# Attention of a graph layer by pairs of graphs: four-row-tile scores, and DRAM transposes whose read is issued apart from the write

## Chip, cores and metric

One core of a Trainium2 chip runs the whole program. The metric is the device time of one execution in microseconds, as the median of the runs. All data is float32. A float32 matmul of the program stands as two MATMUL and two LDWEIGHTS instructions in the trace, so counts in the profile are twice those of the code.

## The reference

There are 128 graphs of 128 nodes with 256 features, and an adjacency matrix of 0 and 1 for each. Two layers follow each other. Layer 0 is a graph attention network and a feed-forward block; layer 1 is a relational attention with 8 heads of 32 and four relations, and another feed-forward block:

```python
h = _gat(_gat(x, adj, W1, a1), adj, W2, a2)        # layer 0, softmax over masked scores
h = _layernorm(x + h); x = _layernorm(h + relu(h @ w_ff1 + b_ff1) @ w_ff2 + b_ff2)
...
q, k = heads(src @ Wq + bq), heads(src @ Wk + bk)  # layer 1
attn = softmax(q @ k^T / sqrt(dh))                 # 8 heads, 128 x 128 per graph and head
for r in range(4):
    v_r = heads(src @ Wv[r] + bv[r])
    out = out + (attn * (adj_matrix == r)) @ v_r
x = _ln(src + out @ Wo + bo)
x = _ln(x + gelu(x @ W1 + b1) @ W2 + b2)
```

With adjacencies of 0 and 1 alone the relations 2 and 3 select nothing, and the kernel takes its BINARY branch: one mask and two value tensors per graph. A GENERAL branch for other adjacencies is in the program and does not run here.

## The kernel before

**Tiling.** The 128 graphs are 32 groups of `G` = 4. A group goes through five stages, each a Python generator: `load`, `gat` (two graph attentions), `ff0`, `att` (the attention of layer 1) and `ff1`. The token tile `y` has 128 nodes on the partitions and 4 x 256 features.

**Order of the work.** `layers` keeps a heap of due times. Group g starts a stage at 100·g plus the `begin` of the stage, in units of its own; each `yield TIMES[...]` says after how many units the stage goes on. The emission order that comes out of the heap is pinned for TensorE (from unit 280 on) and for SyncE (from 0 on), which issues every DMA. TensorE and SyncE therefore work through a list in a fixed order, each at the speed that its waits allow; a unit is no time on the chip. The order on VectorE, ScalarE and GpSimd is left to the compiler's scheduler. In the steady state five groups are in flight, each in another stage.

**Transposes by DRAM.** Away from the first and last groups, a transpose of a 128 x 1024 tile is a 32 x 32 block transpose on VectorE (L288), four DMAs of 128 KB that write the blocks to a DRAM tile `zd` (L291), and one DMA of 512 KB that reads it back in the new order (L293). `transposed` issues all five in a row on SyncE; the read waits there until the writes have landed. `features` makes the transposed features `hT` of a group this way for `ff0`, `att` and `ff1`, and `turned` does it for the attention weights `e` of a graph. `gat_weighting` sends one row of sums through DRAM in the same manner (L405, L407).

**Attention.** `qT` and the keys come from `hT` by L468 and L474. The keys are written twice by ScalarE into the constant tiles `kbd` (L476), each time with the rows of every other head multiplied by zero, so that one 64-row tile of TensorE serves two heads: the scores of a graph are 4 matmuls of 64 rows x 256 columns (L490), two row tiles at a time, into two PSUM banks. `weights(b)` then takes maxima (VectorE, L496), 8 exponentials with sums (ScalarE, L500), reciprocals (L501) and the product on GpSimd (L502). `by_relation` masks the transposed weights (L515), `values` makes the value tensors (L531, L532), `weighted` sums over 32-column tiles, four at a time (L544), and L577/L578 apply `Wo` and add to `y`. The graphs of a group are staggered: `weights(b + 2)` stands right behind `weighted(b)`.

**The second half of a feed-forward block** is L378, in three blocks of TensorE work, the last of which closes `y`; `normalised` (L256 to L265) follows, and then the next stage's `features`. PSUM has 7 banks under the name `mm` and one under `av`.

## Time and profile before

| what | value |
|---|---|
| median of 3 runs (range) | 2890.71 us (2889.82 to 2892.4) |
| the profiled execution | 2891.83 us; its span 2890.0 us |
| TensorE matmul / weight load busy | 2787.7 us (96%) / 2166.1 us (75%) |
| VectorE / ScalarE / GpSimd busy | 1504.7 / 1724.3 / 1597.4 us (52 / 60 / 55%) |
| DMA queue, share of 16 engines | 49.1% |
| L490, scores: union of matmuls | 147.7 us, x1024 |
| L544, weighted sums: union of matmuls | 107.3 and 104.6 us, x2048 each |

Busy time is a union over the span; a matmul's end is modelled, so that the start of one block and the start of the next say more than the durations. "PE" is TensorE's matmul, "PEld" its weight load, "SPq" SyncE's issuing of DMAs. In a timeline view the columns are start and duration in us, engine, line, operation, output and inputs, shape and count, and in brackets the idle time before it with what ended it.

### The profile page before, as it was taken

How to read it: one execution, taken by the hardware profiler on the slowest of the kernel's cores; microseconds unless marked ns; L12 is line 12 of the kernel's file. 1: busy time of each engine (PE TensorE's matmuls, PEld its weight loads, DVE VectorE, ACT ScalarE, POOL GpSimd, SP SyncE). 2: the span in 40 equal slices, each digit the busy share in tenths (PEclk: the TensorE clock that was granted, in tenths of full speed). 3: DMA queues.
4: the chain of work that ended last, by engine and by line, in shares of the span. 5: the costliest groups of instructions: out<-in, count | busy, mean ns of one | idle time of the engine just before them, and what ended most of it. 6: DMA issues, size and time to landing. Idle time of an engine off the chain costs nothing.

```text
span 2890.0 us, 45554 instructions
## 1 busy us (share of the span) xinstructions
PE 2787.7 (96%) x15554; PEld 2166.1 (75%) x15554; DVE 1504.7 (52%) x3072; ACT 1724.3 (60%) x5191; POOL 1597.4 (55%) x1866
## 2 busy tenths in 40 slices
PE   4996999999999999999999999999999999999988
PEld 3764777777877777777777787777778777777756
DVE  5444545545545555554554555555565545555442
ACT  3445566566666666666656666666666675666543
POOL 1434556556655556665655665565566565556553
PEclk7998999999999999999999999999999999999999
DMA  7145454555554556555445545454654544564310
GB/s 275 45 104 121 104 118 106 110 132 127 119 114 107 113 117 139 114 119 118 106 108 131 129 113 125 104 111 117 137 128 107 123 106 111 122 135 106 77 37 15
DMA packets 1156945, 328.69 MB, mean 114 GB/s; under 512 B 903008, under 2 KB 1126752, under 8 KB 1156064
## 3 DMA queue, kind: packets, MB, share of 16 engines
q1 hardware_dynamic: 1156704, 325.68, 49.1%
q8 instruction: 126, 2.06, 0.3%
q14 instruction: 115, 0.94, 0.1%
HBM read 195.97 MB, written 129.62 MB: 113 GB/s over the span
## 4 chain that ended last, share of the span: by engine, by line
PE 71%; DMA 7%; DVE 6%; POOL 5%; ACT 4%; issue 2%; SPq 2%; DVEq 0%; POOLq 0%; ACTq 0%
PE mm L378 25%; PE mm L333 19%; PE mm L531 5%; PE mm L474 4%; PE mm L468 4%; PE mm L490 4%; PE av L544 3%; PE mm L435 3%; PE mm L577 3%; POOL tok L271 2%; DMA zd<-e 2%; SPq L291 2%; DMA eT<-zd 2%; PE mm L454 1%; DMA zd<-T 1%
## 5 line engine op out<-in xcount | busy, mean ns | idle before, releaser
L271 POOL TENSOR_TENSOR tok<-tok,ln_rows 128x512 f32<-128x512 f32 (+1 forms) x596 | 669.5, 1133 | 34.4 <-PE mm L282 11.1
L500 ACT ACTIVATE e<-mm,nm 128x128 f32<-128x128 f32 x1024 | 362.1, 397 | 239.2 <-DVE nm L496 229.6
L378 PE MATMUL mm<-w,fT 128*128 128x256 f32 x2048 | 460.6, 381 | 0.0
L378 PE MATMUL mm<-wf,fT 128*128 128x256 f32 x2048 | 456.6, 381 | 1.5 <-ACT fT L354 1.5
L378 PEld LDWEIGHTS mm<-w,fT 128*128 128x128 f32 x2048 | 386.6, 190 | 74.2 <-issue 24.2
L502 POOL TENSOR_TENSOR e<-e,s 128x512 f32<-128x512 f32 x256 | 269.4, 1053 | 300.5 <-DVE s L501 299.8
L378 PEld LDWEIGHTS mm<-wf,fT 128*128 128x128 f32 x2048 | 386.5, 190 | 64.3 <-issue 9.2
L515 DVE TENSOR_TENSOR m<-eT,am 128x1024 f32<-128x1024 f32 x128 | 186.2, 1454 | 385.2 <-DMA eT<-zd 374.8
L496 DVE TENSOR_REDUCE nm<-mm 128x4 f32<-128x512 f32 x256 | 162.9, 676 | 254.6 <-PE mm L490 254.6
L265 ACT ACTIVATE tok<-tok,nmr,rstd 128x256 f32<-128x256 f32 x480 | 249.9, 603 | 20.1 <-POOL nmr L263 20.0
L531 PE MATMUL mm<-wv,T 128*128 128x512 f32 x512 | 249.3, 610 | 0.0
L352 POOL TENSOR_TENSOR fT<-fT 128x512 f32<-128x512 f32 x128 | 163.3, 1277 | 153.8 <-ACT fT L351 153.8
L500 ACT ACTIVATION_READ_ACCUMULATOR e<-mm,nm 128x1 f32 x1024 | 242.9, 237 | 0.0
L354 ACT ACTIVATE fT<-fT,col 128x512 f32<-128x512 f32 x256 | 170.4, 715 | 118.8 <-DVE fT L348 117.1
L309 POOL TENSOR_TENSOR t<-T 128x256 f32<-128x256 f32 x64 | 47.6, 744 | 321.3 <-DMA T<-zd 321.0
L333 PE MATMUL mm<-T,w 128*128 128x256 f32 x768 | 202.3, 386 | 4.0 <-DMA T<-zd 2.9
L424 POOL TENSOR_TENSOR e<-e,s 128x512 f32<-128x512 f32 (+1 forms) x68 | 68.1, 1002 | 244.4 <-DVE s L423 230.6
L333 PE MATMUL mm<-T,wf 128*128 128x256 f32 x768 | 193.1, 381 | 0.0
L256 DVE BATCH_NORM_STATS2 st<-tok 128x6 f32<-128x256 f32 x480 | 176.7, 409 | 2.4
L333 PEld LDWEIGHTS mm<-T,w 128*128 128x128 f32 x768 | 144.4, 192 | 30.6 <-issue 6.5
L422 ACT ACTIVATE e<-e,nm 128x128 f32<-128x128 f32 x256 | 101.6, 430 | 105.2 <-DVE nm L419 98.8
L333 PEld LDWEIGHTS mm<-T,wf 128*128 128x128 f32 x768 | 146.1, 191 | 21.7 <-issue 0.8
(144 smaller groups left out, 5147.1 us busy)
## 6 DMA issues: line engine op xcount, KB each, us to landing
zd<-e SPq DMA_DIRECT2D x496, 128.0 KB, 4.6
eT<-zd SPq DMA_DIRECT2D x124, 512.0 KB, 4.4
zd<-T SPq DMA_DIRECT2D x364, 128.0 KB, 3.5
T<-zd SPq DMA_DIRECT2D x91, 512.0 KB, 4.2
xt<-in_xT_dram SPq DMA_DIRECT2D x32, 512.0 KB, 5.0
e<-zsd SPq DMA_DIRECT2D x60, 256.0 KB, 3.3
tok<-in_x_dram SPq DMA_DIRECT2D x30, 512.0 KB
out_dram<-tok SPq DMA_DIRECT2D x29, 512.0 KB, 5.4
```

Source lines behind the costliest of these rows:

```text
L256: nc.vector.bn_stats(st, y[:, b])
L265: nc.scalar.activation(y[:, b], y[:, b], AF.Identity, bias=nmr[:, b:b + 1], scale=rstd[:, b:b + 1])
L271: engine.tensor_tensor(y[:, b:b + n], y[:, b:b + n], v[:, None, :].to_broadcast([P, n, D]), op)
L333: nc.tensor.matmul(p[:, i], win[k][:, ts(f0 + i, P)], hs[k], start=first and i == 0, stop=True, skip_group_check=True)
L352: nc.gpsimd.tensor_add(hi[:, :, 1], hi[:, :, 1], hi[:, :, 0])
L354: nc.scalar.activation(lo[:, i], lo[:, i], func, bias=bin_[:, f0 + i:f0 + i + 1])
L378: nc.tensor.matmul(ys[b // 2][:, b % 2], fT[f][:, ts(b, N)], wout[:, f], start=b % 2 == 0 and n == 0, stop=n == FC - 1, skip_group_check=True)
L496: nc.vector.tensor_reduce(nm, p, AX.X, OP.max, negate=True)
L500: nc.scalar.activation(eh[:, q], p[:, q], AF.Exp, bias=nm[:, q:q + 1], accum_out=s[:, q:q + 1])
L502: nc.gpsimd.tensor_mul(eh, eh, per_row(s, N))
L515: nc.vector.tensor_tensor(m, eT, at[:, b][:, None, :].to_broadcast([P, H, N]), OP.mult)
L531: nc.tensor.matmul(p, hT[:, b, f], wv[:, f, r:r + 2], start=f == 0, stop=f == DC - 1)
```

## The change

1. Attention works on pairs of graphs (`together` = 2): `weights`, `turned`, `weighted` and the `Wo` product take two graphs at a time. A group has two steps in place of four, and the second pair's scores stand right behind the first pair's weighted sums.
2. The keys are written once, to a tile `kT`; `kbd`, `own` and `bk_own` go. The scores are 8 matmuls per graph of 32 rows x 128 columns, one per head, in four row tiles with a PSUM bank each; a pair uses four banks of `mm`.
3. `transposed` is split into `put` (block transpose and writes) and `get` (the read). The read is issued 7 units after the writes; a pair's second read 3 units after its first. In `gat_weighting` the read comes 5 units after the write.
4. Due times change: 48 units from a pair's scores to its weighted sums, `gat` and `load` begin 10 units earlier, row and attention of the graph attention network have 13 and 22 units, and the leads of `ff0`, `att` and `ff1` are cut by the 7 units that `put` takes. `m` has two buffers.

```diff
-    "ff first half": 10, "ff half": 5, "row": 16, "gat": 19, "wh": 5.5,
-    "gat copy": 2, "qk": 4.5, "scores": 5.5, "turn0": 10, "turn1": 5,
-    "v0": 5.5, "av": 9, "v": 4, "wo": 4, "turn": 3, "mask": 3,
-    "lead ff0": 26, "lead att": 32, "lead ff1": 32, "affine": 7,
+    "ff first half": 10, "ff half": 5, "row": 13, "gat": 22, "wh": 5.5,
+    "gat copy": 2, "qk": 7, "scores": 18, "mask": 7, "av": 13, "wo": 8, "turned": 10,
+    "put": 7, "next put": 3, "row put": 5,
+    "lead ff0": 19, "lead att": 25, "lead ff1": 25, "affine": 7,
...
-    period=100, bufs=dict(T=5, tok=5, m=1, mm=7, v=2),
-    begin=dict(load=-87, gat=-51, ff0=48, att=132, ff1=300),
+    period=100, bufs=dict(T=5, tok=5, m=2, mm=7, v=2),
+    begin=dict(load=-97, gat=-61, ff0=48, att=132, ff1=300),
...
-        nc.sync.dma_start(t, s.rearrange("k p i t -> p k (i t)"))
+        return s
+
+    def get(t, s):
+        if s is not None:
+            nc.sync.dma_start(t, s.rearrange("k p i t -> p k (i t)"))
...
-        transposed(y.rearrange("p b (c f) -> p (b c) f", f=P), blocks, direct, blocks)
+        s = put(y.rearrange("p b (c f) -> p (b c) f", f=P), blocks, direct, blocks)
+        yield TIMES["put"]
+        get(blocks, s)
...
-            for q in range(2):
-                nc.scalar.activation(c.kbd[i][:, :, q], p, AF.Identity, scale=c.own[:, q:q + 1],
-                                     bias=c.bk_own[q][:, i:i + 1])
+            nc.scalar.activation(kT[:, i], p, AF.Identity, bias=c.col["bk"][:, i:i + 1])
...
+            scores = [ps.tile([P, n, DC, N], F32, name="mm") for _ in range(HC)]
+            for j, b in enumerate(bs):
+                for i in range(DC):
+                    for q in range(HC):
+                        rows = ts(q, DH)
+                        nc.tensor.matmul(scores[q][:, j, i], qT[rows, i, ts(b, N)], kT[rows, i, ts(b, N)],
+                                         start=True, stop=True, tile_position=(q * DH, 0))
...
+        es = weights(range(STEP))
         yield TIMES["scores"]
+        eT = yield from turned(es)
+        for b in range(0, G, STEP):
+            bs = range(b, b + STEP)
+            vs = [values(k) for k in bs]
+            affine(y, "02", b, STEP)
+            yield TIMES["mask"]
+            parts = [(by_relation(k, e, range(R)), v) for k, e, v in zip(bs, eT, vs)]
             yield TIMES["av"]
+            oT = weighted(parts)
+            if b + STEP < G:
+                es = weights(range(b + STEP, b + 2 * STEP))
             yield TIMES["wo"]
+            p = ps.tile([P, STEP, D], F32, name="mm")
+            for j in range(STEP):
+                for i in range(DC):
+                    nc.tensor.matmul(p[:, j], oT[:, j, i], c.wo[:, i], start=i == 0, stop=i == DC - 1)
+            nc.vector.tensor_add(y[:, b:b + STEP], y[:, b:b + STEP], p)
+            if b + STEP < G:
+                yield TIMES["turned"]
+                eT = yield from turned(es)
```

## The prediction

> **What bounds the kernel now.** I read the page's busy times first, then the waits of TensorE, the windows of a period's length, and the timelines of the engines in one period.
>
> ```profile
> PE 2787.7 (96%) x15554; PEld 2166.1 (75%) x15554; DVE 1504.7 (52%) x3072; ACT 1724.3 (60%) x5191; POOL 1597.4 (55%) x1866
> ...
> PE mm L443 <- POOL e L424: 16.2, 4, 8.9
> PE av L544 <- DMA eT<-zd: 14.6, 2, 12.0
> ...
> 170.00:255.00 85.00, 64.16 (x404) 42.46 (x404) 37.57 (x72) 37.06 (x137) 19.80 (x25) 0.90 0.50 110
> ...
> 340.00:425.00 85.00, 85.00 (x482) 66.42 (x481) 44.27 (x93) 53.60 (x162) 50.02 (x58) 1.00 0.52 116
> ...
> 2805.00:2890.00 85.00, 66.51 (x338) 54.03 (x336) 22.12 (x49) 32.24 (x67) 33.38 (x42) 0.90 0.09 25
> ```
>
> TensorE is busy all the time and waits for others in a handful of places. From 340 to about 2690 us a window of 85 us holds 85.00 us of matmuls at a granted clock of 1.00; only the filling (20.8 us idle between 170 and 255) and the end have holes. No other engine passes 54 of 85 us. So in the middle the order list of TensorE sets the time, and what shortens it shortens the kernel, until a wait appears.
>
> ```profile
> 1403.62 7.07 PE L378 MATMUL mm<-w,fT 128*128 128x256 f32 x32
> 1410.62 1.14 PE L490 MATMUL mm<-kbd,T 64*128 64x256 f32 x8
> 1411.68 0.43 PE L544 MATMUL av<-eT,v 128*32 128x128 f32 x8
> 1411.92 0.40 PE L544 MATMUL av<-m,v 128*32 128x128 f32 x8
> 1412.14 0.40 PE L544 MATMUL av<-eT,v 128*32 128x128 f32 x8
> 1412.36 0.40 PE L544 MATMUL av<-m,v 128*32 128x128 f32 x8
> 1412.69 1.14 PE L490 MATMUL mm<-kbd,T 64*128 64x256 f32 x8
> 1413.76 3.72 PE L378 MATMUL mm<-w,fT 128*128 128x256 f32 x16
> ```
>
> Starts are read here, not durations. A full-array instruction of 256 columns takes 7.00/32 = 0.218 us (1403.62 to 1410.62). A graph's scores take 1.06 us (1410.62 to 1411.68; 1412.69 to 1413.76) for 8 instructions that run two abreast, so 4 rounds of 0.218 and 0.19 of filling and emptying. A graph's weighted sums take 1.01 us (1411.68 to 1412.69) for 32 instructions, four abreast: 0.22 us per 8, so 0.109 per round of four, and 0.14 besides.
>
> **One period, added up.** A group has 240 instructions of L333 and L378 (52.0 us), 6.9 for L468 and L474, 6.9 for L531, 3.5 for L577, 7.0 for the graph attention, 4.2 of scores and 4.0 of weighted sums: 84.5. The block of the same kind starts again 85.05 us later (1403.62 and 1488.67), so about 0.6 us goes to the four places per period where the full array gives way to smaller tiles and comes back, 0.15 each.
>
> **The edits on TensorE.** *Scores.* A pair has 32 instructions of 32 rows and 128 columns in four row tiles, 8 rounds. Four column tiles do a round in 0.109 us (L544), and the full array holds that pace with 128 columns of weights per instruction too:
>
> ```profile
> 124.72 0.94 PE mm L282 x8
> ```
>
> So a pair costs 8 x 0.109 + 0.19 = 1.06 us where two graphs cost 2.12: 2.1 us less per group. No row shows four row tiles. Its bounds are rounds of four at 0.109 (1.06 per pair) and one instruction after another (32 x 0.109 + 0.19 = 3.7 per pair, 3.1 us more per group); I take the first, since L490 does run its two row tiles abreast, weight loads too. A rule speaks against taking all of it: the Trainium skill, "TensorE: Matmul & The Clock Gate", section "Measured speedup vs the span model", gives four row tiles 3.07 times the speed of one instead of 4. By that, as an estimate, a pair would take 1.33 us and 0.5 us less would be saved per group; the sum goes by the rows above.
>
> *Weighted sums.* A pair is one block of 16 rounds: 16 x 0.109 + 0.14 = 1.88 instead of 2.02, 0.28 us per group. *Changes of tile size.* By the due times the second pair's sums (unit 67) stand right before the next group's first scores (71), and the first pair's sums right before the second pair's scores (19): two departures from the full array, not four, 0.3 us. Together 2.7 us: a period of 85.05 - 2.7 = 82.35.
>
> **Edits off TensorE.** The keys' copies fall from four per group to two (L476: 92.6 us busy in all, so 46 less on ScalarE); maxima and exponentials stay in number, reciprocals halve, GpSimd's product is one of twice the size. None of it is on the path while ScalarE has 31 us free per period. What it does is make bursts: 16 exponentials for a pair.
>
> ```profile
> 1412.51 0.37 ACT L500 ACTIVATE e<-mm,nm 128x128 f32<-128x128 f32 x1 [5.94 <-DVE nm L496]
> ...
> 1412.87 0.36 ACT L500 ACTIVATE e<-mm,nm 128x128 f32<-128x128 f32 x1
> ```
>
> One follows another by about 0.35 us, the first 1.9 us after the scores start. So a pair's four banks are held for 1.9 + 16 x 0.35 = 7.5 us. TensorE's list behind the first scores is half of the last feed-forward part (3.5), L577 (1.7), the first visit of the next one (1.7), the other half (3.5): the visit that needs the fifth and sixth bank comes 11.4 us after them. 3.9 us of cover; I charge nothing. If it fails (the graph attention's exponentials, 1.5 us, can come ahead, and more), each us over is paid once per period, 28 us in all. The rule that row tiling raises the pressure on PSUM (the Trainium skill, "TensorEngine Tiling (Array Packing)", "Gotcha 1: PSUM Pressure") speaks for such a wait; no row of this trace shows one, and by the rule alone no sum can be made.
>
> From a pair's scores to its sums TensorE has 37 to 41 us of other work. The chain needs 1.9 + 5.6 of exponentials, 2.1 (L502 twice), 1.2 (L288), 4.6 and 4.4 to land, 2 x 1.45 (L515): 22.7. Covered.
>
> **The trips in two steps.** SyncE no longer stands waiting for writes to land before it goes on; no stall of TensorE is due to that, so nothing is gained in the middle. But the order changes at one place. The due times give: taken modulo the period of 100, the writes of the next group's features are due at 32 (`begin` 132), the writes of the second pair's weights at 37 (132 and the yields 7, 25, 7, 18, 7, 3, 7, 13, 8, 10, which make 237), the read of those features at 39 (132 and 7). Eight more writes now stand between the features' writes and their read. In the profile:
>
> ```profile
> 1466.37 1.21 DVE L288 STREAM_TRANSPOSE T<-tok 128x1024 f32<-128x1024 f32 x1
> ...
> 1467.60 2.24 SPq L291 DMA_DIRECT2D zd<-T  x4
> 1472.05 0.38 SPq L293 DMA_DIRECT2D T<-zd  x1
> 1472.48 0.58 SPq L248 DMA_DIRECT2D am<-in_adjT_dram  x1
> 1473.17 4.28 SPq L291 DMA_DIRECT2D zd<-e  x4
> ...
> 1481.80 3.60 PE L468 MATMUL mm<-T,wq 128*128 128x512 f32 x8
> ```
>
> `ff0`'s last L378 ends at 1456.0 and L468 starts 25.8 us later. Of these the features' transpose ends after 11.6, the read is issued 4.5 us after that and lands 4.2 later (page, part 6): 20.3, so 5.5 us of slack. With the change TensorE's list between the two is L577 (1.7), L454 (1.7), the visits of the other feed-forward block (12.1), L435 (3.5) and L531 (3.4): 22.4 us. Writes right behind writes I bound by 2.2 us (this first group of four) and 4.3 (the next): 4.4 to 8.6 for eight, so the read lands 2.2 + 4.4 + 4.2 = 10.8 to 15.0 us after the transpose. The transpose itself takes at least 0.9 (add), 1.9 (statistics), 1.75 (GpSimd), 2.1 (L265) and 1.2 = 7.9 us, and took 11.6 here, in part because VectorE's L515 stood ahead, waiting for its DMA; that wait moves elsewhere. The sum is 18.7 to 26.6 against 22.4: from no stall to 4.2 us per period. I take 9 and 14.1: 23.1, a stall of 0.7.
>
> **Filling and end.** Between 85 and 340 us 27 us are idle, mostly single graphs waiting one after another for their weights' trip; two pairs wait twice, not four times, but longer. Bounds 15 either way, and I take 6 us of gain. At the end 27 us are idle from 2720 on; a pair's chain is longer with nothing beside it: 5 us of gain to 15 of loss, taken as 4 of loss.
>
> **Sum.** 28 periods x (2.7 - 0.7) = 56; the groups at both ends bring about half of 2.7 x 4 = 5; filling and end 2. The profiled execution took 2891.8 us, 1.1 above the median: 2890.7 - 63 = 2828.
>
> **Rivals.**
> *The features' read is late* (slower). Mechanism as above, SyncE's order; it decides from 2.7 us per period. At 4.2 us the middle loses 28 x 1.5 = 42: 2926. For it: the eight writes are certain. Against: the transpose must be as late as before.
> *The gain is mostly eaten*, by the same read at 1.7 to 2.5 us or by ScalarE's bursts holding banks: 28 x 0.2 to 1.0 left, 2855 to 2883.
> *The row tiles don't run four abreast.* Two abreast a pair takes 16 x 0.109 + 0.19 = 1.93, and 0.9 is left per period: with the stall of 0.7, 2878. One by one: 2.5 us more per period and the stall, 2980.
> *All waits are covered and the filling gets its 15 us:* 28 x 2.7 + 5 + 15 = 95: 2796.
>
> **Chances.** The forecast, 2800 to 2855: 0.55. Below: 0.08. Mostly eaten: 0.15. Late read, slower: 0.14. Row tiles: 0.08, half of it slower. A measurement tells 0.2% (6 us) from no change; 0.03 of the eaten and late cases lies within it. Faster 0.78, same 0.03, slower 0.19. The range 2795 to 2900 leaves out 0.07 below and 0.13 above.
>
> **What would show it.** Right: L490's successor at about 1.06 us per pair, its four row tiles starting together; L544's at 1.88; two departures from the full array per period; L468 about 82 to 83 us after the one before; waits of L468 for "DMA T<-zd" under 1 us each. Wrong: row tiles following each other; L468 idle for 3 us and more in every period, with eight writes between the features' write and read on SyncE; L333 waiting for ScalarE.

## The result, and the profile after

The changed kernel takes 3167.1 us (median of 4 runs, 3161.1 to 3171.0) against 2891.6 us for the kernel before in the same measurement: a ratio of 1.095, interval 1.093 to 1.097. The forecast was 2828 us, in a range of 2795 to 2900. It was wrong in sign and far outside its range. Of the four runs of one variant below, e13, one took 9181 us, three times as long as the others, and its figures are those of the other three.

From here on lines are those of the changed kernel: L470 (q) and L475 (k) were L468 and L474, L491 the scores, L557 the weighted sums, L584 the `Wo` product, L285 and L291 the writes and the read of a transpose, L282 VectorE's block transpose, L504 the exponentials, L507 GpSimd's product, L250 to L259 the normalisation, L265 its scaling on GpSimd. L333 to L388, the feed-forward block, kept their numbers.

Where the time went, counted between the third and the thirtieth start of the q product: 27 periods take 2567.5 us after and 2301.2 before, so 95.1 us instead of 85.2, and 266 us are lost there. The third start itself comes 5.4 us earlier (282.8 against 288.2), and what follows the thirtieth, which still holds two more starts, is 18.2 us longer. That is the whole difference of the spans, 3169.2 against 2890.0 us.

TensorE's waits, after (us in total, times, longest). In the kernel before, the first did not occur and the second came to 0.9 us:

```profile
PE mm L470 <- DMA T<-zd: 137.3, 28, 6.3
PE mm L333 <- ACT fT L351: 92.3, 43, 3.4
```

The stretch of 340 to 2600 us in the view of windows, after. Of 2260 us TensorE is busy for 2052 (before: 2256), and the granted clock is 0.96 instead of 1.00. No other engine has become full; ScalarE's 1242 us are the most.

```profile
340.00:2600.00 2260.00, 2052.43 (x12206) 1583.11 (x12205) 1093.63 (x2098) 1242.25 (x3753) 1130.09 (x1185) 0.96 0.50 105
```

TensorE's timeline after, in the place that answers to the one shown of before (start, duration, and in brackets the idle time ahead):

```profile
1466.05 1.13 PE L333 MATMUL mm<-t,wf 128*128 128x256 f32 x4 [2.56 <-ACT fT L351]
...
1488.31 1.89 PE L584 MATMUL mm<-wo,oT 128*128 128x256 f32 x8
...
1516.96 6.40 PE L470 MATMUL mm<-T,wq 128*128 128x512 f32 x8 [5.86 <-DMA T<-zd]
1523.19 3.60 PE L475 MATMUL mm<-T,wk 128*128 128x512 f32 x8
...
1535.51 1.17 PE L491 MATMUL mm<-kT,T 32*128 32x128 f32 x32
1536.61 3.72 PE L378 MATMUL mm<-w,fT 128*128 128x256 f32 x16
```

Three readings. The 32 score instructions of a pair end 1.10 us after they start (1535.51 to 1536.61): the four row tiles run abreast, and the weighted sums ahead of them took 1.89 us (from 1533.62). So scores and weighted sums cost what was forecast. But L470 waits 5.86 us for its transposed features, and then takes 6.23 us to L475, where eight instructions of the same form take 3.43 us a line later (L475, to the L378 that starts at 1526.62). The group L470 as a whole:

```profile
L470 PE MATMUL mm<-T,wq 128*128 128x512 f32 x256 | 183.2, 881 | 137.3 <-DMA T<-zd 137.3
```

881 ns per instruction, against 592 before and 592 for L475. The windows show the granted clock (the number after the five engines) at 0.55 in the six microseconds after the idle stretch, then at 1.00 again.

```profile
1517.00:1523.00 6.00, 6.00 (x8) 2.61 (x9) 2.22 (x3) 0.00 (x0) 0.00 (x0) 0.55 1.27 246
1523.00:1529.00 6.00, 6.00 (x21) 3.61 (x20) 1.46 (x2) 2.22 (x5) 0.00 (x0) 1.00 0.52 137
```

Why the features are late is read from the timelines of SyncE, VectorE, GpSimd and ScalarE:

```profile
1501.09 2.67 SPq L285 DMA_DIRECT2D zd<-T  x4
1503.86 7.32 SPq L285 DMA_DIRECT2D zd<-e  x8
1511.23 1.86 SPq L291 DMA_DIRECT2D T<-zd  x1
```

```profile
1488.59 0.69 DVE L388 TENSOR_TENSOR tok<-tok,mm 128x512 f32<-128x512 f32 x1 [0.45 <-PE mm L378]
...
1490.72 0.13 DVE L251 BATCH_NORM_AGGREGATE mv<-st 128x2 f32<-128x6 f32 x1
...
1499.81 1.25 DVE L282 STREAM_TRANSPOSE T<-tok 128x1024 f32<-128x1024 f32 x1 [0.15 <-ACT tok L259]
```

```profile
1490.89 1.90 POOL L507 TENSOR_TENSOR e<-e,s 128x1024 f32<-128x1024 f32 x1 [3.61 <-DVE mv L251]
1492.87 0.23 POOL L253 TENSOR_SCALAR rstd<-mv 128x4 f32<-128x4 f32 x1
1493.18 0.23 POOL L255 TENSOR_SCALAR nmr<-mv 128x4 f32<-128x4 f32 x1
1493.37 1.90 POOL L507 TENSOR_TENSOR e<-e,s 128x1024 f32<-128x1024 f32 x1
1495.23 1.04 POOL L256 TENSOR_TENSOR rstd<-rstd,mhalf 128x4 f32<-128x4 f32 x1
1496.24 1.28 POOL L265 TENSOR_TENSOR tok<-tok,ln_rows 128x512 f32<-128x512 f32 x1
1497.46 0.21 POOL L257 TENSOR_TENSOR nmr<-nmr,rstd 128x4 f32<-128x4 f32 x1
```

```profile
1497.71 2.08 ACT L259 ACTIVATE tok<-tok,nmr,rstd 128x256 f32<-128x256 f32 x4 [0.81 <-POOL nmr L257]
```

`ff0`'s last L378 gives way to L584 at 1488.31. The block transpose ends 12.7 us later, the read is issued 10.2 us after that, behind four writes of the features and eight of the pair's weights, and TensorE starts another 5.7 us later: 28.6 us, while TensorE's list between the two holds 22.8. The period is a typical one: over 26 periods the medians are 12.8, 10.2 and 5.4 us, 28.7 in all.

The transpose is late through GpSimd. VectorE has closed the statistics at 1490.85, and transposes as soon as ScalarE's normalisation is done. In between GpSimd's four small operations of the normalisation are 1.7 us of work and take until 1497.67, because the pair's two products (1.90 us each) and a scaling (1.28 us) lie among them.

The second wait, for ScalarE's copy L351, has the same products in its history. A little earlier in the same run, GpSimd has a pair's two products in a row and then a normalisation that is cut by a scaling of another tile:

```profile
1449.48 3.75 POOL L507 TENSOR_TENSOR e<-e,s 128x1024 f32<-128x1024 f32 x2 [3.51 <-DVE s L506]
...
1453.83 1.04 POOL L256 TENSOR_TENSOR rstd<-rstd,mhalf 128x4 f32<-128x4 f32 x1
1454.84 1.27 POOL L265 TENSOR_TENSOR tok<-tok,ln_rows 128x512 f32<-128x512 f32 x1
1456.07 0.20 POOL L257 TENSOR_TENSOR nmr<-nmr,rstd 128x4 f32<-128x4 f32 x1
```

ScalarE, in its timeline, waits for that normalisation (nmr) with feed-forward copies behind it:

```profile
1456.30 2.08 ACT L259 ACTIVATE tok<-tok,nmr,rstd 128x256 f32<-128x256 f32 x4 [2.20 <-POOL nmr L257]
1458.28 0.56 ACT L340 COPY fT<-mm 128x512 f32<-128x512 f32 x1
...
1463.91 1.34 ACT L354 ACTIVATE fT<-fT,col 128x512 f32<-128x512 f32 x2
...
1465.40 1.08 ACT L351 COPY fT<-mm 128x512 f32<-128x512 f32 x2
```

L351 comes at 1465.40, and TensorE, which has wanted its PSUM bank since 1463.5, goes on at 1466.05. Over the whole run ScalarE waits 189 us for nmr ahead of the `tok` normalisations, against 20 before.

How far this wait goes back to nmr can be read from the trace. From the copy that ended each of TensorE's waits for L351, ScalarE's instructions are followed back to the last one ahead of which ScalarE itself stood idle for more than 0.15 us. For 71 of the 92 us this is a `tok` normalisation that waited for nmr. For another 20 us it is L354, the activation of the feed-forward block, which waited for a sum of VectorE (L348).

### The profile page after: what moved, and what is told of

Its sections match the earlier page's. It is cut to its first block, busy times and chain, and to the rows that moved or that the text cites. A ratio compares the mean times of both kernels' runs of the same rounds, so it can differ in the third digit from the quotient of the medians.

```text
span 3169.2 us, 46779 instructions
## 1 busy us (share of the span) xinstructions
PE 2816.0 (89%) x16578; PEld 2173.5 (69%) x16578; DVE 1510.3 (48%) x2873; ACT 1682.8 (53%) x5063; POOL 1529.4 (48%) x1610
## 3 DMA queue, kind: packets, MB, share of 16 engines
q8 instruction: 133, 2.18, 0.3%
## 4 chain that ended last, share of the span: by engine, by line
PE 34%; ACT 21%; POOL 18%; issue 11%; DMA 7%; SPq 5%; DVE 3%; ACTq 0%; POOLq 0%; DVEq 0%
PE mm L378 14%; ACT e L504 7%; POOL tok L265 6%; PE mm L470 5%; DMA T<-zd 5%; SPq L285 5%; POOL e L507 4%; ACT fT L354 4%; POOL rstd L256 4%; ACT tok L259 4%; PE mm L333 3%; PE mm L475 3%; PE av L557 3%; PE mm L542 3%; ACT e L423 1%
## 5 line engine op out<-in xcount | busy, mean ns | idle before, releaser
L265 POOL TENSOR_TENSOR tok<-tok,ln_rows 128x512 f32<-128x512 f32 x476 | 618.5, 1320 | 20.8 <-PE mm L276 12.8
L378 PE MATMUL mm<-w,fT 128*128 128x256 f32 x2048 | 460.7, 381 | 0.0
L378 PE MATMUL mm<-wf,fT 128*128 128x256 f32 x2048 | 456.7, 381 | 1.5 <-ACT fT L354 1.5
L378 PEld LDWEIGHTS mm<-w,fT 128*128 128x128 f32 x2048 | 386.6, 190 | 67.4 <-issue 13.9
L378 PEld LDWEIGHTS mm<-wf,fT 128*128 128x128 f32 x2048 | 386.4, 190 | 57.5 <-ACT fT L354 1.9
L507 POOL TENSOR_TENSOR e<-e,s 128x1024 f32<-128x1024 f32 x128 | 241.4, 1897 | 343.2 <-DVE s L506 269.0
L504 ACT ACTIVATE e<-mm,nm 128x128 f32<-128x128 f32 x1024 | 358.2, 394 | 46.2 <-DVE nm L495 45.8
L259 ACT ACTIVATE tok<-tok,nmr,rstd 128x256 f32<-128x256 f32 x480 | 249.1, 589 | 200.7 <-POOL nmr L257 189.3
L470 PE MATMUL mm<-T,wq 128*128 128x512 f32 x256 | 183.2, 881 | 137.3 <-DMA T<-zd 137.3
L526 DVE TENSOR_TENSOR m<-eT,am 128x1024 f32<-128x1024 f32 x128 | 176.8, 1397 | 184.0 <-DMA eT<-zd 183.5
L542 PE MATMUL mm<-wv,T 128*128 128x512 f32 x512 | 240.7, 615 | 0.0
L504 ACT ACTIVATION_READ_ACCUMULATOR e<-mm,nm 128x1 f32 x1024 | 240.3, 235 | 0.0
L470 PEld LDWEIGHTS mm<-T,wq 128*128 128x128 f32 x256 | 70.8, 289 | 233.9 <-DMA T<-zd 144.3
L476 ACT ACTIVATE kT<-mm,col 128x512 f32<-128x512 f32 x64 | 43.9, 687 | 326.4 <-PE mm L475 326.4
L333 PE MATMUL mm<-T,w 128*128 128x256 f32 x768 | 196.3, 384 | 0.7 <-ACT T L280 0.2
L333 PE MATMUL mm<-T,wf 128*128 128x256 f32 x768 | 192.8, 381 | 0.0
L561 ACT COPY oT<-av 128x512 f32<-128x512 f32 x64 | 37.4, 585 | 276.9 <-PE av L557 276.9
L360 ACT ACTIVATE fT<-mm,col 128x256 f32<-128x256 f32 x256 | 107.2, 472 | 137.8 <-PE mm L333 97.8
```

Of the source, the lines that this page charges most:

```text
L259: nc.scalar.activation(y[:, b], y[:, b], AF.Identity, bias=nmr[:, b:b + 1], scale=rstd[:, b:b + 1])
L265: engine.tensor_tensor(y[:, b:b + n], y[:, b:b + n], v[:, None, :].to_broadcast([P, n, D]), op)
L333: nc.tensor.matmul(p[:, i], win[k][:, ts(f0 + i, P)], hs[k], start=first and i == 0, stop=True, skip_group_check=True)
L378: nc.tensor.matmul(ys[b // 2][:, b % 2], fT[f][:, ts(b, N)], wout[:, f], start=b % 2 == 0 and n == 0, stop=n == FC - 1, skip_group_check=True)
L470: nc.tensor.matmul(p, c.wq[:, f, ts(i, P)], hT[:, :, f], start=f == 0, stop=f == DC - 1)
L504: nc.scalar.activation(e[:, k], p[:, j, i], AF.Exp, bias=nms[q][:, j, i:i + 1], accum_out=s[:, k:k + 1])
```

## The experiments

Diffs are against the changed kernel unless said otherwise. "Period" is the mean of the same 27 periods; "late read", "copies" and "banks" are TensorE's waits in us for the features at the q product, for ScalarE's L346 and L351 together, and for the exponentials L504 that hold PSUM banks (in e4 and e11 the lines that answer to these); "q busy" is the busy time of the q product (115 us at full clock).

| kernel | us | ratio to before | period | late read | copies | banks | q busy |
|---|---|---|---|---|---|---|---|
| before | 2891 | 1 | 85.2 | 0 | 1 | 0 | 115 |
| changed | 3167.1 | 1.093–1.097 | 95.1 | 137 | 92 | 0 | 183 |
| e1 read first | 3151.8 | 1.088–1.092 | 94.7 | 1 | 101 | 113 | 116 |
| e2 late norm | 3130.6 | 1.080–1.085 | 94.0 | 130 | 85 | 0 | 180 |
| e3 both | 3105.8 | 1.072–1.076 | 93.3 | 3 | 62 | 114 | 118 |
| e5 filler | 3133.1 | 1.081–1.085 | 93.6 | 29 | 99 | 0 | 117 |
| e7 writes early | 3130.8 | 1.081–1.085 | 93.7 | 0 | 197 | 0 | 147 |
| e6 all three moves | 3081.5 | 1.064–1.068 | 92.1 | 0 | 168 | 0 | 139 |
| e9 one step | 3195.3 | 1.103–1.108 | 96.3 | 0 | 85 | 92 | 123 |
| e10 = e6, product on VectorE | 3004.2 | 1.038–1.042 | 89.5 | 2 | 97 | 0 | 122 |
| e12 = e6, small pieces | 3072.5 | 1.061–1.066 | 91.7 | 2 | 157 | 0 | 133 |
| e13 = e10, scaling later | 2988.8 | 1.032–1.037 | 88.8 | 3 | 98 | 0 | 122 |
| e14 = e13, normalisation on VectorE | 2983.7 | 1.028–1.034 | 89.0 | 2 | 109 | 0 | 124.5 |
| e15 = e13, product emitted late | 3039.7 | 1.050–1.056 | 90.5 | 7 | 44 | 0 | 117 |
| e16 = e6, product emitted late | 3073.5 | 1.061–1.065 | 92.0 | 0 | 171 | 0 | 124 |
| e4 row tiles alone | 2912.4 | 1.005–1.009 | 86.0 | 0 | 4 | 14 | 115 |
| e11 row tiles alone, spaced | 2905.8 | 1.004–1.008 | 85.8 | 0 | 13 | 1 | 115 |

**e1_read_first: the read of the features ahead of the eight writes.** The attention's read is issued 4 units after its writes and no longer 7.

```diff
-    def features(y, direct):
+    def features(y, direct, wait=TIMES["put"]):
...
-        yield TIMES["put"]
+        yield wait
...
-        hT = yield from features(y, first or direct)
+        hT = yield from features(y, first or direct, 4)
...
-        yield TIMES["lead att"]
+        yield TIMES["lead att"] + 3
```

> The changed kernel, with the features' read of the attention stage issued 4 units after the writes instead of 7 (and the lead 3 units longer), so that on SyncE it stands ahead of the eight writes of the second pair's weights. Nothing else moves. Theory A (the read stands behind eight writes on SyncE, TensorE's L470 waits 4.9 us per period for it and then runs at half the clock, 2.4 us more): the wait of L470 for the DMA falls from 137 us to under 30 and L470's busy time from 183 us to about 115; 28 x 7.3 = 205 us less, about 2960 us. Rival B (the features' transpose itself is late, because VectorE, ScalarE and GpSimd work in bursts of two graphs): the read leaves earlier but the wait falls by less than half, and the time stays above 3080 us. The wait for ScalarE's L351 (92 us) stays in both.

The late read is gone as the theory has it (137 to 1 us), and the slow q product with it (183 to 116). The time fell by 15 us only: a wait of nearly the same size stands in another place. TensorE's waits in this run:

```profile
PE mm L333 <- ACT e L504: 113.4, 27, 4.5
PE mm L333 <- ACT fT L351: 101.2, 53, 3.4
```

The read is now issued 5.3 us after the transpose instead of 10.2 (medians), and the transpose ends no earlier. So without the eight writes ahead of the read L470 has no wait, but taking that wait away is worth little by itself.

**e2_late_norm: the attention's closing normalisation 19 units later.**

```diff
-        yield 1
+        yield 20
         normalised(y)
```

> The changed kernel, with the normalisation that closes the attention stage due 19 units later (95 in place of 76), so that its 2.1 us on ScalarE leave the visits of the next feed-forward block. Nothing else moves. Theory C (the waits of L333 for ScalarE's L351, 92 us in all, come from ScalarE's fixed order: a normalisation that waits for GpSimd stands ahead of the copies that TensorE needs): these waits fall to under 30 us, and the time to about 3167 - 70 = 3095 us. Rival D (the burst of 16 exponentials alone makes ScalarE late): the waits stay above 70 us and the time within 20 us of 3167. The wait of L470 for its DMA stays at 4 to 5 us per period in both.

37 us faster, but not for the reason given: the wait for the copies hardly fell (92 to 85). The theory that this one normalisation holds ScalarE up is refuted as the main cause. Where the 37 us come from is only in part visible: the late read, the copies and the q product together fall by 18 us.

**e3_read_first_late_norm: both edits.**

> Both edits of the two runs before. If the two waits are all that keeps the changed kernel from its shorter list on TensorE (82.4 us per period), the time is 2890 - 28 x 2.7 + some 10 for the ends = 2825 us, and half of the remaining small waits give 2840. If only the first is removed, about 2960. If a third wait comes up where these two were (the second pair's weights arrive later on SyncE, behind the features' trip, and the weighted sums L557 wait for them), 2900 to 2960 with that wait named in the profile.

61 us faster than the changed kernel. It shows where e1's new wait comes from. ScalarE's timeline:

```profile
1515.45 1.28 ACT L411 ACTIVATE e<-e,wh 128x128 f32<-128x128 f32 x4 [11.79 <-DMA e<-zsd]
...
1521.83 0.35 ACT L504 ACTIVATE e<-mm,nm 128x128 f32<-128x128 f32 x1
```

ScalarE works in its compiled order, and ahead of the 16 exponentials of a pair it has L411, which waits for a row of the graph attention. That row has been ready on VectorE since 1488.9, but its write (L405) stands on SyncE behind the eight writes of weights, two reads and the next features' writes:

```profile
1492.61 8.39 SPq L285 DMA_DIRECT2D zd<-e  x8
...
1508.94 0.70 SPq L405 DMA_DIRECT2D zsd<-zs  x1
```

The scores were done at about 1512.8; the exponentials start at 1521.8. TensorE runs out of PSUM banks meanwhile:

```profile
1523.36 2.07 PE L333 MATMUL mm<-T,wf 128*128 128x256 f32 x4 [4.12 <-ACT e L504]
```

This is the failure of cover that the prediction named, by way of SyncE: the eight writes hold up whatever stands behind them, and when the features' read no longer does, the graph attention's row does.

**e5_filler: nine more matmuls of 256 columns ahead of the q product**, on constants, into a bank that nobody reads.

```diff
+        if binary and 2 <= g < NG - 1:
+            fill = ps.tile([P, 2 * P], F32, name="mm")
+            for k in range(9):
+                nc.tensor.matmul(fill, c.wq[:, 0, :P], c.wq[:, 0], start=k == 0, stop=k == 8)
```

> The changed kernel with 9 extra matmuls of 256 columns (18 instructions, 3.9 us, result unused) put right before L470, in the time in which TensorE waits for the features. Theory E (an idle TensorE of 5 to 6 us brings the granted clock to half, and L470 pays it with 881 ns per instruction in place of 592): with under 3.4 us of idle time left, L470 goes back to about 115 us busy, the clock of the steady state to 1.00, and the time falls by about 28 x 2.4 = 67 us to 3100, though more work was added. Rival F (L470 is slow because the read of the features is still landing, or because of its operands): L470 keeps 180 us and the time stays at 3167 or rises.

Adding 117 us of work made the kernel 34 us faster. The q product (L474 here) after its shortened wait:

```profile
1504.21 3.67 PE L474 MATMUL mm<-T,wq 128*128 128x512 f32 x8 [0.49 <-DMA T<-zd]
```

Its busy time is 117 us instead of 183, and the granted clock from 340 to 2600 us is 0.99 instead of 0.96. That the idle stretch, not the data, makes L470 slow is thereby shown. The gain is half of what was expected although 66 us come off the q product: filler and wait together (117 + 29 us) are 9 us more than the wait had been, so 57 us are left; of these 34 arrive, and the waits for the copies take 7 of the others.

**e7_writes_early: the second pair's eight writes ahead of the features' writes.**

```diff
-            yield TIMES["mask"]
+            yield TIMES["mask"] + (5.5 if b else 0)
...
-                yield TIMES["turned"]
+                yield 4.5
```

> The changed kernel with the second pair's writes due at 31.5 instead of 37, just ahead of the features' writes at 32 (the 5.5 units are put back before the masks, so that the weighted sums keep their place). The second pair's transposes end 4 to 5 us before the features' transpose, so the eight writes can leave while SyncE would only wait. Theory G (SyncE's one order is the cause: the eight writes behind the features' writes delay all that follows, first the features' read, and behind it the row of the graph attention, for which ScalarE waits ahead of the exponentials): the wait of L470 for its DMA falls under 20 us, no new wait of L333 for L504 comes up as it did when the read alone was moved, and the time falls to about 3167 - 28 x 7 = 2970 us. Rival H (the transposes and trips of two graphs in one burst are late wherever they stand): a wait of over 80 us stays at L470, L333 or L557, and the time is above 3080 us.

No wait for a DMA is left at L470 and none for banks, and 36 us are gained. But the wait for the copies doubles, from 92 to 197 us.

**e6_writes_early_read_first_late_norm: the three moves together.**

> The changed kernel with all three moves of due times: the second pair's writes at 31.5, the features' read at 36, the attention's normalisation at 95. Theory G: the row of the graph attention arrives before the scores, the wait of L333 for L504 (114 us with the other two moves) falls under 30 us, and the time to about 3106 - 28 x 5 = 2960 or below; with nothing left but small waits, 2850 to 2900. Rival H: the wait of L333 for L504 stays above 80 us and the time above 3060 us.

3081 us: the waits for DMAs are out of the middle of the run, 86 of 276 us are back, and the largest wait left is TensorE's for ScalarE's copies, with the half clock that follows (q busy 139). Putting SyncE's order right gives back less than a third of the loss.

**e9_one_step: the trips as they were**, with no units between write and read, and these units added to the leads and to the row and mask times instead.

> The changed kernel with the trips through DRAM in one step again: every read due with its writes (no units between), the units put back behind it. Theory G: the features' read no longer stands behind the eight writes, L470's wait goes (137 us) and its clock comes back, but the eight writes and the waits for their landing still stand ahead of the row of the graph attention, so that ScalarE waits for it as when the read alone was moved: about 3150 us, with the wait on L333 for L504. If the two steps are of use by themselves, it is above 3167 us; if they are the whole harm, under 2950 us.

28 us slower than the changed kernel, with another wait: L584 waits 64 us in all for ScalarE's copies of the weighted sums (L561). So the split into two steps is of use, and the loss lies in what the two kernels share: the pairs and the due times that go with them. No run takes these two apart.

**e4_rows_alone: the kernel before with nothing but the four row tiles, per graph.** `kbd` becomes `kT`, and per graph 16 instructions of 32 rows and 128 columns (as the trace counts them) replace 8 of 64 rows and 256 columns; maxima are taken four times per graph instead of twice.

> The kernel before with the four-row-tile scores alone: keys written once, 8 matmuls of 32 rows x 128 columns per graph in four row tiles and four banks, everything else (graphs one by one, due times, trips in one step) as before. From the changed kernel's trace a pair's scores take 1.10 us, 8 rounds, so a single graph should take 4 x 0.109 + 0.2 = 0.64 us instead of 1.06: 1.7 us per period, 48 us in the middle, about 2843 us, if four banks per graph cost no wait. If the four banks, each half used, make TensorE wait (L333 for ScalarE's exponentials), the gain is lost and the time is 2880 or more.

Slower by 0.7%, where a gain of 48 us was expected if banks cost nothing. Three of a group's four score blocks fall from 1.06 to 0.66 us; the fourth stands right behind another one and must wait for banks:

```profile
1423.45 0.88 PE L483 MATMUL mm<-kT,T 32*128 32x128 f32 x4
1424.55 0.48 PE L483 MATMUL mm<-kT,T 32*128 32x128 f32 x2 [0.21 <-ACT e L495]
1425.24 0.71 PE L483 MATMUL mm<-kT,T 32*128 32x128 f32 x10 [0.21 <-ACT e L495]
1425.88 2.43 PE L372 MATMUL mm<-w,fT 128*128 128x256 f32 x10
```

It takes 2.43 us (1423.45 to 1425.88): four half-used banks per graph instead of two.

**e11_rows_alone_spaced: e4, the second scores moved on** (`scores` 8, `turn0` 7.5).

> The kernel before with the four-row-tile scores alone, and the second graph's scores due 2.5 units later (76.5 in place of 74; its transpose stays). In the run without the delay three of four score blocks took 0.66 us instead of 1.06, and the fourth took 2.43 us, because it came 1.7 us after another one and waited for ScalarE to empty PSUM banks. With the block behind half of the feed-forward part (3.5 us later) the banks are free: 4 x 0.4 = 1.6 us less per period than before, 45 us, about 2846 us. If the wait only moves to the matmuls behind it, 2880 to 2900.

Now all four blocks take 0.66 us and no score waits, and 1.6 us of work per period are saved; yet the period is 85.8 against 85.2. TensorE idles 1.2 us per period in the middle (32 of 2260 us) against 0.1 before, mostly small waits for ScalarE. Another 1.1 us lies in the matmuls of the feed-forward blocks, which take that much longer from start to start at a granted clock of 1.00; their cause stays open. So even this gain does not survive in this order of work.

**e10_product_on_vector: e6 with the product L507 on VectorE.**

```diff
-                nc.gpsimd.tensor_mul(e, e, per_row(s, N))
+                nc.vector.tensor_mul(e, e, per_row(s, N))
```

> The kernel with all three moves of due times (3081 us), and the product of the attention weights with their reciprocal sums (L507, 241 us on GpSimd, 1.9 us each) done by VectorE instead. Theory I (with the DMA waits gone, ScalarE stands in its fixed order at normalisations that wait for GpSimd, 239 us in all, and TensorE's copies L346 and L351 stand behind them; GpSimd is late because its instructions come in lumps of two graphs): the wait of ScalarE for GpSimd's nmr falls below 100 us, TensorE's waits for L346 and L351 from 168 us to under 80, and the time by 28 x 4 = 110 us to about 2970. Rival J (the compiler's order on ScalarE is what is wrong, and the burst of 16 exponentials; GpSimd's load is no cause): the time stays within 30 us of 3081.

77 us faster than e6, the largest single step of all, and the wait for the copies falls from 168 to 97 us. But ScalarE's wait for nmr hardly changes (239 to 233 us), so the link that the theory gave is not the whole of it; the theory had asked for waits under 80 and 100 us and a gain of 110.

**e12_small_lumps: e6 with the product in two halves per graph and the scaling per graph.**

> The kernel with all three moves of due times (3081 us), with GpSimd's work cut back to the sizes of the kernel before: the product in two halves of 512 per graph, each as soon as its four exponentials are done, and the affine step one graph at a time. GpSimd's total stays. Theory I in the form that the size of the pieces counts: the wait of ScalarE for GpSimd's nmr falls below 150 us and the time below 3050 us. If only the total or the place of the work counts, it stays within 20 us of 3081.

9 us faster than e6, and ScalarE's wait for nmr stays at 232 us (239 in e6). That the size of GpSimd's pieces is the cause is refuted.

**e13_affine_later: e10, with the attention's scaling emitted behind the masks.**

> e10_product_on_vector with one line moved: GpSimd's scaling of a pair's y in the attention is emitted after the pair's weights are masked, not right after its value tensors. Theory J: this two-graph operation of GpSimd (about 1.3 us a piece, two per pair) stands in the middle of another group's normalisation, and ScalarE's normalisation, which its fixed order puts ahead of the feed-forward copies, waits for it. Then ScalarE's wait for nmr falls from 233 us to under 150, TensorE's waits for L346 and L351 from 97 to under 50, and the time from 3004 to about 2960. Rival K: where GpSimd's pieces lie doesn't matter, ScalarE's own order of 16 exponentials and copies does: the waits stay within 20 us of those of e10 and the time within 20 us of 3004.

The wait for nmr fell to 196 us, the time by 15 us, the wait for the copies not at all: the rival's figures for time and copies.

**e14_normalisation_on_vector: e13, with three of the normalisation's four GpSimd operations on VectorE.**

> e13_affine_later, and the three small operations of the normalisation other than the power (L253, L255, L257) on VectorE in place of GpSimd. Theory J': GpSimd's part of the normalisation chain is what ScalarE waits for; with one operation left there ScalarE's wait ahead of L259 falls under 120 us and the time by 20 to 40 us below e13's. Rival K: ScalarE only waits there because it has nothing else in its order; the wait moves to VectorE's result in the same size, and the time stays within 15 us of e13's. Rival L: two more changes of engine per normalisation lengthen the chain: slower than e13 by 10 us or more.

ScalarE's wait for nmr falls to 122 us, 2 us above what the theory asked, but the time by only 5, with the runs of the two variants overlapping (2973 to 2990 us against 2986 to 2993): the rival's figure. The wait has moved to VectorE's own queue. Its timeline has, between the closing sum of `ff0` and the first small operation of its normalisation, the pair's reciprocals, products and transposes:

```profile
1505.64 0.63 DVE L388 TENSOR_TENSOR tok<-tok,mm 128x512 f32<-128x512 f32 x1
...
1514.36 0.15 DVE L253 TENSOR_SCALAR rstd<-mv 128x4 f32<-128x4 f32 x1
```

**e15_product_emitted_late and e16_product_emitted_late_gpsimd: the reciprocals and products emitted with the transposes,** in e13 and in e6.

```diff
-                nc.vector.reciprocal(s, s)
-                nc.vector.tensor_mul(e, e, per_row(s, N))      # in weights
...
+            for e, s in es:                                     # in turned
+                nc.vector.reciprocal(s, s)
+                nc.vector.tensor_mul(e, e, per_row(s, N))
```

> e13_affine_later, with the reciprocals and products of a pair's weights (L506, L507) emitted with the block transposes that need them, 12.5 to 18 units after the scores, not right behind the exponentials. Theory M: the two graphs' chain comes out as one block of 5 us that is emitted ahead of ff0's closing normalisation and so is put ahead of it (in e14_normalisation_on_vector 8.7 us pass from the closing sum L388 to the first small operation of the normalisation, with the reciprocals, products and transposes between them); ScalarE's copies of the next visit stand behind that normalisation. Then ScalarE's wait for nmr falls from 196 to under 100 us, TensorE's waits for L346 and L351 from 98 to under 40, and the time from 2991 to 2940 or less. Rival K: the emission order isn't what delays the normalisation, or the visit has the same wait from another operation: time within 15 us of 2991.

> e6_writes_early_read_first_late_norm with the same late emission, the product staying on GpSimd. Theory M: most of the 77 us that e10 gained came from the product leaving GpSimd's list ahead of the normalisation; emitting it later gains the same way, 40 us or more: 3040 or less, with TensorE's waits for L346 and L351 falling from 168 to under 100. Rival N: it was GpSimd's 1.9 us per product in itself: within 15 us of 3081.

Both miss. e15 halves the wait for the copies (98 to 44 us), which was the aim, and is 51 us slower: another features' read is late now, that of the feed-forward block.

```profile
PE mm L333 <- DMA T<-zd: 68.0, 21, 5.9
```

e16 stays within 8 us of e6, as its rival had it, although ScalarE's wait for nmr falls from 239 to 122 us. With size and place in the emission order ruled out, what is left of GpSimd's product is its 1.9 us of work.

## Why the prediction was wrong

**Two of the three TensorE terms were right.** Scores 1.06 us forecast, 1.10 measured; weighted sums 1.88 and 1.89. Four row tiles keep the pace of 0.109 us per round. The estimate of 1.33 us was not met here; it came from the factor of 3.07 that the Trainium skill, "TensorE: Matmul & The Clock Gate", section "Measured speedup vs the span model", gives for 512 columns, where this case has 128. The third term, 0.3 us for fewer changes of tile size, had no ground: 240 instructions at 7.00/32 = 0.219 us are 52.5 us and not 52.0, so the period's sum leaves nothing for it. No saving of the kind is seen: the instructions of L378 take 28.0 us per period in both kernels. TensorE's list between the features and L470 was forecast at 22.4 us and holds 22.8. At the two ends the forecast was near: the third start comes 5.4 us earlier, where the filling was put at 6, and what follows the thirty-second start is 3.0 us longer, where 4 were taken. The other 15.2 of the 18.2 us behind the thirtieth start lie in the two periods up to the thirty-second.

**The failed step is the chain to the features' read.** Its mechanism, a read behind eight writes in SyncE's order, was named, and it was priced at a stall of 0.7 us per period: 23.1 us of chain (9 and 14.1) against 22.4 of list. The chain took 28.6, and the stall is 5.9 us in the period shown and 137.3 / 28 = 4.9 on average, over the worst case of 4.2. The term that was furthest off is the first: 9 us were taken to the end of the transpose and 12.7 passed, more than the 11.6 of before, which I had thought the upper end. The wait behind VectorE's L515 did go, as argued. But GpSimd's part, put at 1.75 us, took 6.8 (1490.85 to 1497.67), with the pair's two products and a scaling among the four small operations; in the kernel before its median was 3.3. That products of twice the size make GpSimd late for the normalisation was nowhere in the sum. From the transpose to the issue 10.2 us passed, which is near the 9.9 that were taken (14.1 less 4.2). For the landing 4.2 were taken, the median of part 6 of the page, and TensorE started 5.7 us after the issue. The issue by itself lasted 1.86 us here against 0.38 for the read of before; when the data had landed the trace doesn't say.

**A term was missing: the half clock.** A stall of 5.9 us costs more than its length. The q product behind it runs at a granted clock of 0.55 and costs (183.2 - 115.2) / 28 = 2.4 us more per period. This step of the sum was not made at all. The page of the Trainium skill that was cited for the row tiles, "TensorE: Matmul & The Clock Gate", has a section on it, "HAM oscillation — how this bites in real kernels": by it a matmul stream with idle gaps of more than about 3.4 us falls back to half clock each time. The trace agrees in the effect (592 to 881 ns per instruction); on the threshold see below.

**ScalarE was charged at nothing, and that was wrong, though not by the mechanism named.** In the changed kernel itself no matmul waits for banks that exponentials hold; that wait is only there once the features come first (e1, e3: 113 us, about 4.2 each). What the changed kernel pays is the copy L351, 92.3 / 28 = 3.3 us per period. "31 us free per period" was read as cover for bursts, but ScalarE works in a fixed order, and what counts is which result the next entry waits for: its time behind GpSimd's nmr rose from 20 to 189 us.

**The sum made again.** Over the 27 periods, counted from start to start and without waits, TensorE's work was 85.1 us per period before. The scores fell from 4.26 to 2.21 us and the weighted sums from 4.11 to 3.77, together 2.4: 82.7 are left. TensorE is idle for 8.8 us per period: 4.9 of it is the stall, 3.3 the copies, and 0.6 smaller waits. The q product takes 2.4 us more at half clock. All other matmuls take 1.2 us more from start to start than before, 0.4 of it at half clock by the clock records; for the remaining 0.8, mostly in blocks that stand right behind a wait, I have no cause. This makes the 95.1 us measured.

**The rivals.** "The features' read is late" was the right one, at a chance of 0.14. It priced at 4.2 us per period what cost 4.9 + 2.4 = 7.3: a stall that was too short, without the clock. And it could not have been the whole: with the features' read in time (e1, e7) the kernel is still at 3131 to 3152 us. Some of the rivals' figures don't fit the sum's own terms: "mostly eaten" should end at 2878 and not 2883, and row tiles one by one come to 2973 and not 2980, both for the 7 us of the ends; slower adds up to 0.18 at most; and the windows of the middle hold 84.4 to 85.0 us of matmuls, not 85.00 throughout.

**What is shown and what is open.** Shown by runs: L470's wait goes when the read no longer stands behind the eight writes (e1, e7); the half clock at L470 goes when the idle stretch is filled (e5); the wait for PSUM banks, which ScalarE's wait for a row behind the eight writes brings on (e3), goes when those writes are issued earlier (e6); 77 us are gained when GpSimd no longer has the products of pairs (e10), and their size (e12) and place (e16) are not what counts. Read from traces alone: that GpSimd's products make the features' transpose late, and that ScalarE's copies are late because normalisations stand ahead of them. The second of these can't be the whole. ScalarE's wait for nmr was brought from 239 to 122 us in steps (e10, e13, e14) while TensorE's wait for the copies stayed at 97 to 109. Followed back as above, of these waits 52 us in e13 and 29 in e14 lead to a normalisation that waits for nmr, but 44 and 49 to L354, which waits for VectorE's sum L348, and in e14 another 31 to the copy L346, which waits for TensorE itself. No run moved that sum. The last 92 us between e14 and the kernel before (89.0 against 85.2 us per period) have no cause that a run has shown. Most repairs of one wait raised another, and no variant came below the kernel before.

## What to carry over

Work in larger batches halves the number of steps and doubles each burst; on a machine with fixed orders on every queue, the price is on whatever stands next in line on the queues off the critical path, so follow each burst through every queue, and let a worst case exceed the slowest example of the trace. Price a stall of TensorE at its length and at the slow clock behind it: here half as much again. An order that keeps TensorE at 99.8% is worth more than 2.7 us of shorter work per period.

## What the hardware showed unexpectedly

- Half clock does not follow from the length of a single gap. In the clock records of the changed kernel it comes in stretches of 3.41 us (19 times) or twice that (23 times), and a few times in longer ones. After 5.9 us of idle time the eight instructions of the q product take 6.2 us; in e7 after a gap of 3.36 us four instructions take 0.96 us and L470 its full-speed 3.4 us, at a granted clock of 1.00, while in the same run a gap of 2.18 us is followed by half clock; in e10 after one of 2.81 us four instructions take 2.04 us; in e6 two gaps of 1.93 and 1.83 us within 3 us are followed by 3.5 us for eight instructions that take 1.8 at full clock. The figure of about 3.4 us that the Trainium skill gives for such gaps (same page and section as above) is thus no safe bound in these traces. The two cases of e7 and e10, each a gap and what stands behind it:

```profile
1513.30 1.13 PE L333 MATMUL mm<-t,w 128*128 128x256 f32 x4 [3.36 <-ACT fT L351]
1514.26 3.60 PE L470 MATMUL mm<-T,wq 128*128 128x512 f32 x8
...
1538.81 2.08 PE L333 MATMUL mm<-T,w 128*128 128x256 f32 x4 [2.81 <-ACT fT L346]
1540.85 3.75 PE L333 MATMUL mm<-t,w 128*128 128x256 f32 x8
```

- Useless matmuls in a gap can pay: 117 us of filler brought 34 us.
- Eight writes of 128 KB in a row took 7.3 us on SyncE in one place, 8.4 in another, and issuing the 512 KB read behind them took 1.86 us where it took 0.38 before.
